# The second attention's GpSimd work and transfers in program order, its features loaded in fours ahead of time

## The chip, the core and the metric

The kernel runs on one core of one Trainium2 chip. The metric is the device time of one execution in microseconds, as the median of three runs. The profile comes from one more execution, recorded by the hardware profiler.

## What is computed

Two layers, each with a layer norm, an attention and a mixture of experts whose output gates the attention (`x = x + attention * silu(experts)`), on `x` of 4 batches x 512 tokens x 128. The change touches the second attention only. It has 16 heads of 8 features, and runs the same softmax attention under 16 "channels", which scale the scores of each head by another number:

```python
def wl_step(acc, wl):
    cpm, iw = wl
    m = cpm[None, :, None, None]
    Qw = Q * m
    Kw = K * m
    scores = jnp.einsum('bhqd,bhkd->bhqk', Qw, Kw) * SCALE
    scores = scores * jnp.cos(KERR * scores * scores)
    attn = jax.nn.softmax(scores, axis=-1)
    out = jnp.einsum('bhqk,bhkd->bhqd', attn, V)
    return (acc + out * iw, None)
acc, _ = jax.lax.scan(wl_step, acc0, (cos_pm, interference_weights))
combined = acc / WL_CHANNELS
```

The kernel does not take 16 exponentials of each score. It writes each channel's exponential as a combination of six functions of the unscaled score `s`: three exponentials `e`, `e*e`, `e*e*e` (bank 0), and `s*s`, `s` and 1 (bank 1). Summed over the keys, bank 0 needs every score. Bank 1 does not: sums over keys of `s` and `s*s` are products of q's features (its 8 numbers, their squares, and their pairwise products) with sums over the keys ("forms") that are made once a batch.

## The kernel before

**Stages.** A first norm and its experts (up to about 80 us), the first attention (to about 400 us), the second experts `ffn1` (to 531 us), and then the loop of the second attention, `attn1` (L1542), to the end.

**The loop.** It has 64 steps `i`: batch `b = i // 16`, and in a batch `t = i % 16`; `m = t // 4` is a group of four heads, `k = t % 4` a quarter of the keys. In a step TensorE makes the scores of step `i + 1` (`scores1`, tile `s`, 8 matmuls in bf16) and adds step `i`'s three exponentials into `acc` (12 matmuls, tile `acc`). ScalarE makes `e` and its square from the scores, VectorE the third power (L1531). At `t % 4 == 0` VectorE empties `acc` into bank 0 (L1573). Other matmuls lie between: the mixing of batch `b` and `b - 1` (function `mixing`, L1576: `bank1` at t = 4, 8, 12, 15, `sums1`, `quotients1`, and `output1` of the batch before at t = 9), and the preparation of batch `b + 1` (`prepare1`, L1155: token projections at t = 0, 1, 13, `project` of k and q at t = 2 and 3, forms at t = 5, 7, 10, 11). What is multiplied in one step is evicted and finished (`rest`) in the next.

**Where the operands come from.** `project("k")` and `project("q")` leave k and q with features on partitions. GpSimd splits each into three bf16 parts (L1247, L1250), SyncE writes the parts to DRAM (`kd`, `qd`, L1255) in eight places, which make up the pairs of parts that are multiplied with each other (`MEET`); `operands1` (L1288) reads them back, one group m at a time, with the parts stacked on the partitions: four transfers of 128 KB a group, three buffers each. q itself is written to DRAM twice (L1241), so that `features1` (L1298) can read it shifted by d features: for each m two loads of `rows1` (L1304), four of `rows2` (L1309) and four of `other` (L1310), each 64 KB, and then two products on GpSimd: `rows1`'s second half squared (L1305), and `rows2 * other` (L1311). `bank1(b, m)` multiplies the forms with `rows1` and `rows2`. There is one buffer of `other`, and one place in `rows1` and `rows2` for each m.

**GpSimd's other work in the loop**: the squares of the tokens (L1190), the keys' features `feat` for the forms (L1195 to L1205), the sum of the two products of a group (L1381), the output's gate and residual (L1400, L1401), and the experts' gate (`gate1`, L985 and L986, called at t = 2). ScalarE, VectorE and TensorE each write or read what GpSimd makes: `sizes` reduces the squares on VectorE, `output1` on TensorE takes the sums of L1381.

**What sets the order.** Each engine and SyncE's queue take their instructions one after the other. The order of TensorE, ScalarE and VectorE is the program's own: `mm1`, `act1` and `vec1` call `pin`, which is `keep_in_program_order`. GpSimd's instructions and the transfers are not pinned; the scheduler places them. `features1` is called for all four m at t = 0 of the batch (t = 1 in the first):

```python
if t == int(b == 0):
    if b == 0:
        nc.gpsimd.memset(self.rows1[64:65], 1.0)
    for m in range(4):
        self.features1(b, m)
```

Of the kernel before, what the change touches and what calls it, by code (L numbers as in the profile page):

```python
# [21 lines left out]
P = 128  # L22
# [44 lines left out]

MEET = (((0, 0), (0, 1), (1, 0), (1, 1)), ((0, 2), (2, 0), (1, 2), (2, 1)))

# [20 lines left out]
class Kernel:  # L90
# [124 lines left out]
    def load_second(self, pool):  # L215
# [3 lines left out]
        for w in ("q", "k", "v"):  # L219
            self.w1[w] = pool.tile([P, D], F32, name=f"l1w{w}")  # L220
            nc.sync.dma_start(out=self.w1[w], in_=i[f"L1_attn_W{w}"])

            flat = pool.tile([P, D], F32, name=f"l1b{w}f")
            nc.gpsimd.dma_start(out=flat, in_=i[f"L1_attn_b{w}"].partition_broadcast(P))
            self.wt[w] = pool.tile([P, D], F32, name=f"l1w{w}t")
            self.bt[w] = pool.tile([P, D], F32, name=f"l1b{w}t")
            for to, src in ((self.wt[w], self.w1[w]), (self.bt[w], flat)):
                nc.gpsimd.tensor_copy(
                    to.rearrange("p (m r d) -> p m r d", m=4, r=4),
                    src.rearrange("p (r m d) -> p m r d", m=4, r=4),  # L230
                )
            if w != "v":
                self.b1[w] = pool.tile([P, 1], F32, name=f"l1b{w}")
                nc.gpsimd.dma_start(out=self.b1[w], in_=i[f"L1_attn_b{w}"].unsqueeze(1))
        self.b1["o"] = pool.tile([P, D], F32, name="l1bo")
# [80 lines left out]
    def vec1(self, ins):  # L316
        return self.pin(ins)


# [661 lines left out]
    def gate1(self, pool, acc, name):  # L981

        t = pool.tile([P, 4, D], F32, name=f"th{name}", tag="pr1", bufs=2)
        self.act1(t, acc, AF.Tanh, scale=0.5)
        self.nc.gpsimd.tensor_scalar(t, t, 0.5, 0.5, ALU.mult, ALU.add)  # L985
        self.nc.gpsimd.tensor_mul(acc, acc, t)  # L986

# [167 lines left out]
    def prepare1(self, b, xnT, psum, tag):  # L1155
# [9 lines left out]
        def tokens(w):  # L1165
# [9 lines left out]
            def rest(ps):  # L1175
                if w == "v":
                    self.vec1(nc.vector.tensor_tensor(
                        strip[:, :, :, 18:26], ps.rearrange("p k (h d) -> p k h d", d=D1),
                        bc(self.bt[w].rearrange("p (h d) -> p h d", d=D1), 1, 4), ALU.add,
                    ))  # L1180
                    return
                twice = pool.tile([P, 4 * H1, 2 * D1], F32, name=f"tok{w}{b}", tag="tok")
                t = twice[:, :, 0:D1]
                self.vec1(nc.vector.tensor_tensor(
                    t.rearrange("p (k h) d -> p k h d", k=4),
                    ps.rearrange("p k (h d) -> p k h d", d=D1),
                    bc(self.bt[w].rearrange("p (h d) -> p h d", d=D1), 1, 4), ALU.add,
                ))
                sq = pool.tile([P, 4 * H1, D1], F32, name=f"tsq{w}{b}", tag="tsq")
                nc.gpsimd.tensor_mul(sq, t, t)  # L1190
                now["squares" + w] = sq
                if w == "q":
                    return
                fours = "p (g r) d -> p g r d"
                nc.gpsimd.tensor_copy(  # L1195
                    self.feat[:, :, 0:32].rearrange("p g (r d) -> p g r d", r=4),
                    t.rearrange(fours, r=4),
                )
                nc.gpsimd.tensor_copy(
                    self.feat[:, :, 32:64], sq.rearrange("p (g r) d -> p g (r d)", r=4)  # L1200
                )
                nc.gpsimd.tensor_copy(twice[:, :, D1 : 2 * D1], t)
                for d in range(1, 5):
                    at = ROWS1 + 32 * (d - 1)
                    nc.gpsimd.tensor_mul(  # L1205
                        self.feat[:, :, at : at + 32].rearrange("p g (r d) -> p g r d", r=4),
                        t.rearrange("p (g r) d -> p g r d", r=4),
                        twice[:, :, d : d + D1].rearrange("p (g r) d -> p g r d", r=4),
                    )
            return pe, rest  # L1210
# [12 lines left out]
        def project(w):  # L1223
            def pe():
                ps = psum.tile([P, S], F32, name=f"pj{w}{b}", tag=tag[0], bufs=tag[1])
                self.mm1(ps, lhsT=self.w1[w], rhs=toks, start=True, stop=True)
                return ps
# [6 lines left out]
            def rest(t):  # L1234
                if w == "q":

                    dram = now["dram"] = self.a1d.tile(
                        [H1, 2 * D1, S], F32, name=f"qd{b}", tag="qd"
                    )
                    for k in range(2):  # L1240
                        nc.sync.dma_start(out=dram[:, k * D1 : (k + 1) * D1, :], in_=t)  # L1241
                dram = now["parts" + w] = self.a1d.tile(
                    [H1, 2, 4, D1, S], BF16, name=f"{w}d{b}", tag=f"{w}d"
                )
                for k in range(3):
                    part = pool.tile([P, S], BF16, name=f"part{w}{b}_{k}", tag=f"part{k}")
                    nc.gpsimd.tensor_copy(part, t)  # L1247
                    if k < 2:
                        left = pool.tile([P, S], F32, name=f"left{w}{b}_{k}", tag="left", bufs=2)
                        nc.gpsimd.tensor_sub(left, t, part)  # L1250
                        t = left
                    for x in range(2):
                        for i, pair in enumerate(MEET[x]):
                            if pair[w == "k"] == k:
                                nc.sync.dma_start(out=dram[:, x, i], in_=part)  # L1255
            return pe, rest, evict
# [31 lines left out]
    def operands1(self, b, m):  # L1288

        nc, now = self.nc, self.now1[b]  # L1290
        for w in ("q", "k"):
            src = now["parts" + w].rearrange("(r m) x i d s -> m x r (i d) s", m=4)[m]
            for x in range(2):
                t = self.a1q.tile([P, S], BF16, name=f"{w}{x}_{b}_{m}", tag=f"{w}{x}", bufs=3)
                nc.sync.dma_start(out=t, in_=src[x])
                now[w, x, m] = t

    def features1(self, b, m):  # L1298

        nc = self.nc  # L1300
        src = self.now1[b]["dram"].rearrange("(r m) j s -> m r j s", m=4)[m]
        one, two = self.rows1[:, m], self.rows2[:, m]
        for k in range(2):
            nc.sync.dma_start(out=one[k * 32 : k * 32 + 32], in_=src[:, 0:D1])  # L1304
        nc.gpsimd.tensor_mul(one[32:64], one[32:64], one[32:64])  # L1305
        other = self.a1q.tile([P, S], F32, name=f"other{b}_{m}", tag="other", bufs=1)
        for d in range(1, 5):
            rows = slice(d * 32 - 32, d * 32)
            nc.sync.dma_start(out=two[rows], in_=src[:, d : d + D1])  # L1309
            nc.sync.dma_start(out=other[rows], in_=src[:, 0:D1])  # L1310
        nc.gpsimd.tensor_mul(two, two, other)  # L1311

# [44 lines left out]
    def quotients1(self, b, mm, x):  # L1357
# [15 lines left out]
        def rest(out):  # L1373
            for o in range(2):
# [5 lines left out]
                else:  # L1380
                    self.nc.gpsimd.tensor_add(self.prod1[b, m], self.prod1[b, m], t)  # L1381
        return pe, rest

    def output1(self, b, g1):
# [12 lines left out]
        def rest(po):  # L1397
            y = self.a1.tile([P, 4, D], F32, name=f"y{b}", tag="pr1", bufs=2)
            self.vec1(nc.vector.tensor_tensor(y, po, bc(self.b1["o"], 1, 4), ALU.add))
            nc.gpsimd.tensor_mul(y, y, g1[b])  # L1400
            nc.gpsimd.tensor_add(y, y, self.x[:, b * 4 : b * 4 + 4, :])  # L1401
            for k in range(4):
                nc.sync.dma_start(out=self.tiles_of(self.out, b * 4 + k), in_=y[:, k])
        return pe, rest

    def large1(self, flag):
# [5 lines left out]
        def first():  # L1412
# [3 lines left out]
            ))  # L1416
            nc.gpsimd.partition_all_reduce(every, bounds, P, bass_isa.ReduceOp.max)

# [16 lines left out]
    def end1(self, b, g1):  # L1435
# [4 lines left out]
        x = self.x[:, b * 4 : b * 4 + 4, :]  # L1440
        nc.gpsimd.tensor_mul(y, g1[b], bc(self.b1["o"], 1, 4))
        nc.gpsimd.tensor_add(y, y, x)
        den = psum.tile([P, 4, P], F32, name="dene", tag="prep")
# [36 lines left out]
        def output(k):  # L1480
# [10 lines left out]
            self.vec1(v.tensor_add(y[:, k], r, y[:, k]))  # L1491
            nc.sync.dma_start(out=self.tiles_of(self.out, b * 4 + k), in_=y[:, k])

# [48 lines left out]
    def attn1(self, xnT, g1):  # L1542
# [4 lines left out]
        with tc.tile_pool(name="a1", bufs=2) as self.a1, tc.tile_pool(  # L1547
# [47 lines left out]
            third = function(0, 2, self.e1)  # L1595
            waiting, late, prep = [], [], {}
            large = self.large1(flag)
            for i in range(n):
                b, t = i // 16, i % 16
                if t == 2:  # L1600
                    self.gate1(pool, g1[b], b)
# [5 lines left out]
                if t == 0:  # L1607
                    prep = self.prepare1(b + 1, xnT, psum, ("prep", 1)) if b + 1 < B else {}
                if t == int(b == 0):
                    if b == 0:  # L1610
                        nc.gpsimd.memset(self.rows1[64:65], 1.0)
                    for m in range(4):
                        self.features1(b, m)
                nxt = i + 1 < n
# [453 lines left out]
```

## Time and profile before

| | us |
|---|---|
| three runs, median | 927.83 |
| three runs, lowest and highest | 924.93 and 927.9 |
| the profiled execution, its own time | 925.29 |
| its span, from the first to the last instruction | 923.6 |
| TensorE busy (matmuls) | 855.1 (93% of the span) |
| VectorE busy | 595.7 (65%) |
| ScalarE busy | 519.6 (56%) |
| GpSimd busy | 382.5 (41%) |
| start of the second attention's loop | 531.4 |
| mean granted TensorE clock | 0.973 of full speed |

How to read what follows: PE is TensorE, PEld its weight loads, DVE VectorE, ACT ScalarE, POOL GpSimd, and SPq SyncE's queue of transfers. An instruction is named by its line and by what it writes and reads, "out<-in"; a line can be that of a helper, so that all matmuls stand at L311, all activations at L314. In a timeline, the first two numbers are start and duration, and the bracket at the end is the idle time of the engine ahead of the instruction and what ended it. Instructions in GpSimd's or SyncE's queue are not counted as busy while they issue transfers or wait.

### The profile page before, as it was taken

The numbers are of one execution on the slowest core, as the hardware profiler recorded it, in microseconds if no ns is written. First come the engines' busy times: TensorE is split into PE (matmuls) and PEld (weight loads), VectorE is DVE, ScalarE is ACT, GpSimd is POOL, SyncE is SP. The second block draws the span as 40 slices with busy tenths as digits, with TensorE's granted clock in tenths as the row PEclk, the third lists the DMA queues.
The fourth block names the chain that finished last, engine by engine and source line by source line (L and its number), as shares of the span: only waits on it lengthen the run. The fifth ranks groups of instructions, "written<-read, shape, count | busy, mean of one in ns | idle before, by whom it ended". The sixth has DMA issues, their size and how long they took to land. (4 is left out here: it accounts for less than half of the span.)

```text
span 923.6 us, 19255 instructions
## 1 busy us (share of the span) xinstructions
PE 855.1 (93%) x7660; PEld 528.9 (57%) x7660; DVE 595.7 (65%) x1202; ACT 519.6 (56%) x692; POOL 382.5 (41%) x465
## 2 busy tenths in 40 slices
PE   8998999999999999999999999496968999889996
PEld 4665789888898788866777733132325323422324
DVE  7863776676768788733534377364764786586675
ACT  3434564575656756524332497374853878388780
POOL 7730254544544345640330076313854284432112
PEclk9999999999999999999999999797997999899999
DMA  8402221211212121000041011521142214220000
GB/s 214 126 13 76 80 76 25 81 48 48 80 25 81 27 68 36 1 1 1 1 144 51 1 36 61 158 90 64 39 144 85 71 39 146 83 69 32 1 12 16
DMA packets 76705, 56.60 MB, mean 61 GB/s; under 512 B 40337, under 2 KB 65201, under 8 KB 76609
## 3 DMA queue, kind: packets, MB, share of 16 engines
q1 hardware_dynamic: 74608, 53.89, 19.4%
q0 software_dynamic: 1424, 1.16, 0.6%
q8 instruction: 62, 1.02, 0.4%
q10 hardware_dynamic: 576, 0.26, 0.1%
q14 instruction: 35, 0.28, 0.1%
HBM read 35.36 MB, written 19.92 MB: 60 GB/s over the span
## 5 line engine op out<-in xcount | busy, mean ns | idle before, releaser
L1531 DVE TENSOR_TENSOR e<-e,e 128x1024 f32<-128x1024 f32 x126 | 181.0, 1476 | 85.4 <-ACT e L314 85.3
L311 PE MATMUL acc<-e,strip 128*32 128x512 f32 x1520 | 185.9, 606 | 15.6 <-DVE bank L1573 8.2
L314 ACT ACTIVATE e<-s 128x1024 f32<-128x1024 f32 x126 | 122.1, 1022 | 106.3 <-PE s L311 106.3
L314 ACT ACTIVATE e<-e 128x1024 f32<-128x1024 f32 x126 | 126.3, 1060 | 0.0
L311 PEld LDWEIGHTS acc<-e,strip 128*32 128x32 f32 x1520 | 44.9, 110 | 128.6 <-issue 87.0
L314 ACT ACTIVATE h<-ph 128x1024 f32<-128x1024 f32 x32 | 32.7, 1023 | 87.8 <-PE ph L311 87.8
L311 PEld LDWEIGHTS eo<-w_out,h 128*128 128x128 f32 x512 | 61.7, 194 | 11.7 <-issue 10.4
L314 ACT ACTIVATE pj<-pp 128x512 f32<-128x512 f32 x64 | 38.1, 596 | 49.3 <-PE pp L311 49.3
L311 PE MATMUL eo<-w_out,h 128*128 128x128 f32 x512 | 64.0, 279 | 1.0 <-DVE g L958 0.8
L759 POOL TENSOR_TENSOR t<-t,gate 128x512 f32<-128x512 f32 x32 | 40.8, 1275 | 56.1 <-DVE t L692 41.5
L958 DVE SCALAR_TENSOR_TENSOR g<-eo,gw,g 128x128 f32<-128x128 f32 x112 | 31.5, 345 | 48.7 <-PE eo L311 48.7
L311 PE MATMUL ph<-xnT,w_in 128*128 128x512 f32 x128 | 61.2, 600 | 0.0
L311 PE MATMUL dot<-vone,E 128*128 128x65 f32 x512 | 61.1, 273 | 0.0
L311 PEld LDWEIGHTS dot<-vone,E 128*128 128x128 f32 x512 | 59.8, 192 | 1.1 <-issue 0.8
L711 POOL TENSOR_TENSOR t<-t,gate 128x512 f32<-128x512 f32 x32 | 41.0, 1280 | 33.3 <-DVE t L692 33.3
L1305 POOL TENSOR_TENSOR rows<-rows 32x512 f32<-32x512 f32 x16 | 18.2, 1139 | 86.8 <-DMA rows<-qd 63.7
L311 PE MATMUL s<-q,k 32*128 32x512 bf16 x512 | 39.7, 383 | 13.0 <-DMA k<-kd 11.7
L734 DVE TENSOR_TENSOR mz<-mz,mu 64x512 f32<-64x512 f32 x56 | 38.3, 685 | 18.3 <-PE mu L311 17.7
L654 DVE SCALAR_TENSOR_TENSOR elu<-elu,up 128x512 f32<-128x512 f32 x60 | 42.4, 707 | 7.2 <-ACT up L314 6.4
L760 POOL TENSOR_TENSOR t<-t,t 128x512 f32<-128x512 f32 x32 | 45.8, 1430 | 2.5
L1311 POOL TENSOR_TENSOR rows<-rows,other 128x512 f32<-128x512 f32 x16 | 25.1, 1570 | 49.2 <-DMA other<-qd 20.1
L630 DVE TENSOR_TENSOR E<-sc,cap 128x1024 f32<-128x1024 f32 x32 | 39.0, 1220 | 9.6 <-PE sc L311 7.0
(279 smaller groups left out, 1618.6 us busy)
## 6 DMA issues: line engine op xcount, KB each, us to landing
vd<-vt SPq DMA_DIRECT2D x32, 256.0 KB
vone<-vd SPq DMA_DIRECT2D x64, 128.0 KB
rows<-qd SPq DMA_DIRECT2D x96, 64.0 KB
kd<-partk SPq DMA_DIRECT2D x32, 128.0 KB
qd<-partq SPq DMA_DIRECT2D x32, 128.0 KB
k<-kd SPq DMA_DIRECT2D x32, 128.0 KB
q<-qd SPq DMA_DIRECT2D x32, 128.0 KB
other<-qd SPq DMA_DIRECT2D x64, 64.0 KB
```

The costliest lines, as they stand in the source:

```text
L311: return self.pin(self.nc.tensor.matmul(*args, **kw))
L314: return self.pin(self.nc.scalar.activation(*args, **kw))
L630: self.vec1(nc.vector.tensor_tensor(e.rearrange("p x hp c -> p (x hp) c"), ps.rearrange("p x hp c -> p (x hp) c"), bc(self.cap.rearrange(" ...
L654: self.vec1(nc.vector.scalar_tensor_tensor(t, t, 1.0, up, ALU.min, ALU.add))
L711: nc.gpsimd.tensor_mul(t, t, self.gate)
L734: self.vec1(nc.vector.tensor_tensor(new[half, :, :, p, 0:DK], old[half, :, :, p, 0:DK], ps[half, :, :, p * 64 : p * 64 + 64].rearrange("d ...
L759: nc.gpsimd.tensor_mul(t, t, gate2)
L760: nc.gpsimd.tensor_add(t, t, seg[n]["t1"])
L958: self.vec1(v.scalar_tensor_tensor(acc[b][:, k, :], eo[:, k, :], w, acc[b][:, k, :], ALU.mult, ALU.add))
L1305: nc.gpsimd.tensor_mul(one[32:64], one[32:64], one[32:64])
L1311: nc.gpsimd.tensor_mul(two, two, other)
L1531: self.vec1(self.nc.vector.tensor_mul(t, src[0][pair], src[1][pair]))
```

## The change

All GpSimd instructions and all transfers of the second attention are pinned to program order (`pool1`, `dma1`). The features of group m are loaded at t = 9, 11, 13 of the batch before (m = 0, 1, 2) and at t = 1 of the batch (m = 3); in the first batch at steps 1 to 4. Their two products are issued at the beginning of the step two later (one later in the first steps). q is written to DRAM a third time, once unduplicated (`once`), and features come by one load of `rows1` and one of `other` that repeat the same rows, so 6 transfers for 10. Parts are written with one transfer for all places that take the same part and lie evenly (`STAND`), 5 for each of q and k in place of 8, and operands are read with one transfer for both stacks, 2 for 4. For that the heads stand in another order: the projections use the permuted weights `wt`, and the permuted bias comes in 4 small loads for each of q and k. The gate is at t = 11 instead of 2.

```diff
+STAND = {
+    "q": (((0, 0, 4, 2), (1, 0, 1, 1)), ((0, 1, 4, 2), (1, 1, 2, 1)), ((1, 2, 4, 1),)),
+    "k": (((0, 0, 2, 1), (1, 2, 3, 1)), ((0, 2, 4, 1), (1, 3, 4, 1)), ((1, 0, 2, 1),)),
+}
...
             if w != "v":
                 self.b1[w] = pool.tile([P, 1], F32, name=f"l1b{w}")
-                nc.gpsimd.dma_start(out=self.b1[w], in_=i[f"L1_attn_b{w}"].unsqueeze(1))
+                own = i[f"L1_attn_b{w}"].rearrange("(r m d o) -> m r d o", m=4, r=4, o=1)
+                for m in range(4):
+                    nc.gpsimd.dma_start(out=self.b1[w][m * 32 : m * 32 + 32], in_=own[m])
...
+    def pool1(self, ins):
+        return self.pin(ins)
+
+    def dma1(self, out, in_):
+        return self.pin(self.nc.sync.dma_start(out=out, in_=in_))
...
-                self.mm1(ps, lhsT=self.w1[w], rhs=toks, start=True, stop=True)
+                self.mm1(ps, lhsT=self.wt[w], rhs=toks, start=True, stop=True)
...
-                    dram = now["dram"] = self.a1d.tile(
+                    once = now["once"] = self.a1d.tile([P, S], F32, name=f"qe{b}", tag="qe")
+                    self.dma1(once, t)
+                    twice = now["twice"] = self.a1d.tile(
                         [H1, 2 * D1, S], F32, name=f"qd{b}", tag="qd"
                     )
                     for k in range(2):
-                        nc.sync.dma_start(out=dram[:, k * D1 : (k + 1) * D1, :], in_=t)
+                        self.dma1(twice[:, k * D1 : (k + 1) * D1, :], t)
                 dram = now["parts" + w] = self.a1d.tile(
-                    [H1, 2, 4, D1, S], BF16, name=f"{w}d{b}", tag=f"{w}d"
+                    [2, P, 4, S], BF16, name=f"{w}d{b}", tag=f"{w}d"
                 )
...
-                    for x in range(2):
-                        for i, pair in enumerate(MEET[x]):
-                            if pair[w == "k"] == k:
-                                nc.sync.dma_start(out=dram[:, x, i], in_=part)
+                    for x, at, end, step in STAND[w][k]:
+                        n = len(range(at, end, step))
+                        self.dma1(dram[x, :, at:end:step], bc(part, 1, n))
...
-        for w in ("q", "k"):
-            src = now["parts" + w].rearrange("(r m) x i d s -> m x r (i d) s", m=4)[m]
+        for w in ("k", "q"):
+            src = now["parts" + w].rearrange("x (m r d) i s -> m (r d i) x s", m=4, r=4)[m]
+            t = self.a1q.tile([P, 2, S], BF16, name=f"{w}_{b}_{m}", tag=f"{w}s", bufs=3)
+            self.dma1(t, src)
             for x in range(2):
-                t = self.a1q.tile([P, S], BF16, name=f"{w}{x}_{b}_{m}", tag=f"{w}{x}", bufs=3)
-                nc.sync.dma_start(out=t, in_=src[x])
-                now[w, x, m] = t
+                now[w, x, m] = t[:, x]
 
     def features1(self, b, m):
 
-        nc = self.nc
-        src = self.now1[b]["dram"].rearrange("(r m) j s -> m r j s", m=4)[m]
+        nc, now = self.nc, self.now1[b]
+        once, twice = now["once"][m * 32 : m * 32 + 32], now["twice"][m * 4 : m * 4 + 4]
         one, two = self.rows1[:, m], self.rows2[:, m]
-        for k in range(2):
-            nc.sync.dma_start(out=one[k * 32 : k * 32 + 32], in_=src[:, 0:D1])
-        nc.gpsimd.tensor_mul(one[32:64], one[32:64], one[32:64])
+        self.dma1(one[0:64], bc(once, 0, 2))
         other = self.a1q.tile([P, S], F32, name=f"other{b}_{m}", tag="other", bufs=1)
         for d in range(1, 5):
-            rows = slice(d * 32 - 32, d * 32)
-            nc.sync.dma_start(out=two[rows], in_=src[:, d : d + D1])
-            nc.sync.dma_start(out=other[rows], in_=src[:, 0:D1])
-        nc.gpsimd.tensor_mul(two, two, other)
+            self.dma1(two[d * 32 - 32 : d * 32], twice[:, d : d + D1])
+        self.dma1(other, bc(once, 0, 4))
+
+        def products():
+            self.pool1(nc.gpsimd.tensor_mul(one[32:64], one[32:64], one[32:64]))
+            self.pool1(nc.gpsimd.tensor_mul(two, two, other))
+        return products
...
-            waiting, late, prep = [], [], {}
+
+            steps = {9: 0, 11: 1, 13: 2, 1: 3}
+
+            def features(b, t):
+
+                out = [(0, t - 1)] if b == 0 and 1 <= t < 5 else []
+                if t in steps and (b, t) != (0, 1):
+                    out.append((b + (t > 1), steps[t]))
+                return out
+            waiting, late, prep, products = [], [], {}, []
...
-                if t == 2:
+                if t == 11:
                     self.gate1(pool, g1[b], b)
...
-                if t == int(b == 0):
-                    if b == 0:
-                        nc.gpsimd.memset(self.rows1[64:65], 1.0)
-                    for m in range(4):
-                        self.features1(b, m)
+                while products and products[0][0] <= i:
+                    products.pop(0)[1]()
+                if i == 1:
+                    self.pool1(nc.gpsimd.memset(self.rows1[64:65], 1.0))
+                for fb, m in features(b, t):
+                    if fb < B:
+                        products.append((i + (1 if i < 5 else 2), self.features1(fb, m)))
```

Every other GpSimd instruction of the second attention (L985, L986, L1190 to L1209, L1247, L1250, L1381, L1400, L1401, L1417, L1441, L1442) is wrapped in `pool1`, and the output's transfers are issued by `dma1`.

## The prediction

> **What bounds the kernel now.** I read the page's busy shares first, then the waits, then TensorE's timeline and the queue's beside it. TensorE is busy 93% of the span, so the question is what keeps it from the other 7%. The waits from 531 us (start of the second attention's loop) to the end are few and long (us in total, times, longest):
>
> ```profile
> ACT e L314 <- PE s L311: 106.3, 46, 18.1
> PE po L311 <- POOL pr L1381: 15.7, 4, 11.1
> PE s L311 <- DMA k<-kd: 11.7, 2, 10.9
> PE acc L311 <- DVE bank L1573: 8.2, 8, 2.3
> PE acc L311 <- DVE e L1531: 7.3, 2, 7.0
> ```
>
> In TensorE's timeline (start, duration, instruction, idle before it) these are single places:
>
> ```profile
> 596.30 0.61 PE L311 MATMUL s<-q,k 32*128 32x512 bf16 x4 [10.93 <-DMA k<-kd]
> 638.78 1.92 PE L311 MATMUL acc<-e,strip 128*32 128x512 f32 x4 [7.01 <-DVE e L1531]
> 695.62 0.80 PE L311 MATMUL po<-wo_rep,pr 128*128 128x128 f32 x2 [11.09 <-POOL pr L1381]
> 696.84 5.74 PE L311 MATMUL po<-wo_rep,pr 128*128 128x128 f32 x26 [0.42 <-POOL pr L1381]
> 787.70 0.80 PE L311 MATMUL po<-wo_rep,pr 128*128 128x128 f32 x2 [2.82 <-POOL pr L1381]
> 789.90 5.31 PE L311 MATMUL po<-wo_rep,pr 128*128 128x128 f32 x26 [1.41 <-POOL pr L1381]
> ```
>
> Each ends at work of SyncE's queue or GpSimd that stands in a bad order. At 585 to 596 the operands of group 3 (L1295) are issued behind eighteen part and q transfers of the next batch (576.28 to 589.4); at 690 the sum that the output waits for (L1381) stands on GpSimd behind a feature product whose load has only just been issued; at 632 a vector reduction waits 9.93 us for squares (L1190) that stand behind feature products. The queue before the stall of 695.62:
>
> ```profile
> 682.82 1.37 SPq L1304 DMA_DIRECT2D rows<-qd  x2
> 684.29 0.60 SPq L1309 DMA_DIRECT2D rows<-qd  x1
> 684.93 0.60 SPq L1310 DMA_DIRECT2D other<-qd  x1
> ...
> 688.79 0.60 SPq L1310 DMA_DIRECT2D other<-qd  x1
> ```
>
> And the stretches by time (TensorE, weight loads, VectorE, ScalarE, GpSimd, granted clock, DMA share, GB/s):
>
> ```profile
> 590.00:600.00 10.00, 2.94 (x20) 0.69 (x24) 0.00 (x0) 1.68 (x2) 0.00 (x0) 0.50 0.29 95
> 690.00:700.00 10.00, 3.96 (x17) 3.66 (x18) 0.00 (x0) 0.00 (x0) 3.70 (x3) 0.50 0.27 97
> 720.00:730.00 10.00, 10.00 (x88) 3.29 (x84) 6.16 (x7) 7.94 (x9) 3.81 (x3) 1.00 0.14 49
> ```
>
> In a stall all engines stand still and the clock is 0.50; elsewhere TensorE is full at 1.00 and no other engine is near its limit.
>
> **What the Trainium skill says.** (1) "DMA: Bandwidth & Descriptors", Anatomy of one DMA: a wait for a semaphore happens on the issuing sequencer before dispatch, so a waiting transfer holds all behind it. The trace agrees: the queue's own waits show 12 of L1310 for GpSimd's product, 48.2 us. (2) Same page, Rules for kernel authors: a leading broadcast of c copies confines a transfer to at most c of the 16 engines. No broadcast load of this kind is in the trace, but feature loads, whose source leads with 4 heads, hold the DMA share at 0.27, or 4.3 engines, with 97 GB/s: some 23 GB/s each. (3) "SBUF — State Buffer", Who interferes with whom: a VectorE operation with two SBUF inputs and a GpSimd one that reads SBUF exclude each other. The trace agrees: the product e takes 1226 ns in the median and up to 2332. (4) "TensorE: Matmul & The Clock Gate", What's actually happening: after an idle window of about 3.4 us the clock is half. Above: 0.50 behind both long stalls.
>
> **The yardstick.** I took the start of each step's score matmuls (s, x8) as the step's start; a step does scores and 12 accumulations. Step 9, with nothing else, goes from 575.00 to 578.25: 3.25 us. Added work from the chain's undisturbed rows: token projections 1.09 (three a batch), projections 1.07 (two), forms pl 1.49 (four), bank b 1.92 (four), den 1.87, mix 1.06, po 3.77. So batch 1 needs 16 x 3.25 + 11.37 + 19.43 = 82.8 us, and takes 624.97 to 733.92 = 108.95, 26.1 too long. Batch 2: 92.8, 10.0 too long. Batch 0, without den, mix and po of a predecessor: needs 75.0, takes 93.55, 18.5 too long. Together 54.6. Five steps hold most of it:
> - step 10 (578.25 to 596.30): 18.05 for 3.25 + 1.87 + 1.49 = 6.6: 11.4
> - step 11 (to 604.91): 8.61 for 4.7: 3.9 (the slow clock: its accumulation took 5.28, not 2.78)
> - step 17 (629.31 to 646.47): 17.16 for 3.25 + 1.09 + 1.87 = 6.2: 10.9
> - step 25 (680.57 to 702.51): 21.94 for 3.25 + 3.77 = 7.0: 14.9
> - step 41 (780.91 to 795.14): 14.23 for 7.0: 7.2
>
> Sum 48.3. The other 6.3 of these batches and some 7 in batch 3 are short waits for VectorE.
>
> **The change part by part.**
> - **GpSimd and SyncE in program order; features of m = 0, 1, 2 at t = 9, 11, 13 of the batch before and m = 3 at t = 1, products two steps later.** I followed each queue for batch 1, from the start of t = 1, with durations under contention (page and groups). GpSimd: token products from 2.7 us on, 11.5 long (L1190 1.37, L1195 1.62, L1199 1.28, L1202 0.61, four of L1205 at 1.67), to 14.2; products of m = 3 (1.14 + 1.57), to 16.9; the splits of k 6.0 and q 6.6 and gaps 1.5, to 31; the sums L1381 2 x 1.55, with their input ready at 32, to 35. The output matmuls come at 43.8: 9 us of margin. Forms need the token products at 23.5, ready at 14.2. SyncE waits for the splits up to 31, then issues group 3's operands, landing by 36, wanted at 54. The gate moves from t = 2 to 11; its two products (1.28 + 1.93) lie between y and m = 0's product, and are wanted a batch later. The all-reduce of batch 3 (L1417, idle 9.33 ahead of it) stays between m = 3's product at t = 3 and the sums at t = 7, four steps on: 0. The out transfers stand ahead of the features at t = 11 and wait for y; that costs the queue 8 us, and features of m = 1 still land 1.5 us after their slot at t = 13, where only GpSimd waits. So all five long steps go: **-48.3**.
> - **Broadcast loads.** `one` 128 KB, four `two` of 64 KB, `other` 256 KB: 6 issues for 10. Not in the trace. Lower bound: on all 16 engines at 23 GB/s, 640 KB take 1.7 us. Upper bound: `one` on two engines, the rest on four, engines 0 and 1 carry 64 + 64 + 64 KB: 8.3 us and some 2 of latency. I take the upper one: against 9.7 us or more of two steps it costs GpSimd about a microsecond at times, inside the margin. **0**; if the margin were gone, 1 us a set.
> - **Fewer issues.** Per batch 78 become 49 (features 40 to 24, parts 16 to 10, operands 16 to 8, q 2 to 3) at 0.6 us: 17 us less of SyncE, which TensorE doesn't see: 0, but it lets the queue run ahead. One copy of q more, 256 KB a batch: hidden at 0.14 to 0.3 DMA share.
> - **Batch 0 is tight**, since its four sets go out at steps 1 to 4. GpSimd's token products (538.9 on) now stand ahead of the first feature product, which ended at 550.98 in between: they end at about 550.8, the products at 553.8. Bank 0's second half could start at 551.03: **+2.4**. After that each `other` (one buffer) waits for the last product; the splits fill these gaps; q's last parts leave at 576, group 3's operands land near 581 and are wanted near 586: **+0.5** for the small margin. GpSimd stays busy to 579, so products e stretch in some steps of 3.25 us: **+1.5**.
> - **VectorE loses its rest.** Batch 1's first steps waited 0.2 us after a long stall, batch 2's 2.4 (steps 32 to 36). Batch 1 will look like batch 2: **+2.3**.
> - **At the start**, two biases load in 4 pieces each: 6 more issues on GpSimd at 0.55 = 3.3 us around 15 to 37 us. GpSimd waits 16.0 us at L1130 later: 0 (bounds 0 to 3.3 if the phases' load delays VectorE at 47 us). The permuted weights already exist.
>
> Sum: -48.3 + 2.4 + 0.5 + 1.5 + 2.3 = -41.6. The profiled execution took 925.29 (span 923.6 and 1.7 around it): 883.7. The runs' median, 927.83, lies 2.5 above it, but one of three was below, so I add half: **885**.
>
> **The rivals.**
> - **A: a wait takes the place of the removed ones.** In order, GpSimd waits for a load with splits and sums behind it. Against: 9 us of margin. For: batch 0, and one buffer for `other`. One stall like step 41's per boundary, 2 or 3 x 7: 885 + 18 = 903.
> - **VectorE becomes the bound**: half of a batch's 16 pairs e at 3.5 to 4 us, not 2.4, in steps of 3.25 to 4.3: another 2 to 3 us a batch, 885 + 8 = 893. Against: VectorE is 65% busy.
> - **Slower than before**: the broadcast loads are so slow that every set arrives late. From 9.7 + 9 = 19 us a set (twice my upper bound) TensorE sees it; at 23 us each of 15 sets costs about 3.7, that is 55: 885 + 55 = 940. The 0.27 share with 97 GB/s speaks against it.
> - **The order was not the cause**: the stalls stay for their bytes, 921. At 585 to 596 the share is 0.47, at 686 to 695 0.24, so bytes don't bind.
>
> **Numbers.** Forecast 0.70, A 0.15, VectorE 0.10, slower 0.03, no effect 0.02. Its own range is 876 (nothing of the +6.7 comes, 877.0, and a microsecond of the old short waits goes too) to 893. To 899 it takes in the VectorE case and half of A, and leaves less than 2 in 10. A measurement of this kernel tells about 0.3% from no change. Faster 0.96, within 0.01, slower 0.03.
>
> **What would show it.** Right: no wait of TensorE over 3 us between 531 us and the end; `s` from `k<-kd` and `po` from `pr` gone; clock 1.00 throughout; the loop from its start to the last bank some 332 us for 373. Bank 0 of batch 0 waits 2 us for `rows`. The DMA share in feature loads about 0.2. Wrong: `po` or `b` waits for GpSimd at each batch (A), many short waits for e or bank on VectorE, or a stretch ahead of 531 us that is longer.

## The result and the profile after

| | before | after |
|---|---|---|
| median | 927.57 (4 runs, 924.93 to 927.9) | 889.78 (4 runs, 887.72 to 891.24) |
| ratio, 95% interval | | 0.9597 [0.957, 0.9624] |
| the profiled execution | 925.29 | 890.56 |
| its span | 923.6 | 888.8 |
| start of the loop | 531.42 | 534.06 |
| loop, from the start of step 0 to that of step 62 | 364.2 | 326.6 |
| mean granted clock | 0.973 | 0.992 |

The change is 37.8 us faster in the median; the forecast was 885, so it is 4.8 us short. In the new kernel all lines have moved: matmuls stand at L318, activations at L321, the third power `e` at L1548, bank 0 at L1590, the two products of a group at L1324 and L1325, the sums at L1397, and every pinned transfer at L330.

TensorE's main waits in the new kernel from the loop's start to the end, with two of ScalarE and GpSimd (us in total, times, longest), the counterpart of the first view of the prediction:

```profile
ACT e L321 <- PE s L318: 69.0, 47, 3.5
POOL rows L1325 <- DMA other<-qe: 23.3, 6, 5.1
PE acc L318 <- DVE bank L1590: 10.4, 9, 2.3
PE b L318 <- POOL rows L1324: 1.4, 1, 1.4
PE acc L318 <- DVE e L1548: 1.3, 4, 0.5
PE b L318 <- POOL rows L1325: 1.1, 1, 1.1
```

Before, TensorE waited here for `pr`, `k<-kd`, `bank` and `e`, 11 us at the longest. Now `pr` and `k<-kd` are gone, and no wait of TensorE is longer than 2.3 us. What remains is VectorE: `bank` 10.4 us in nine waits, which stands behind products `e` in VectorE's order. GpSimd waits 23.3 us for `other`; TensorE waits for GpSimd only 1.4 and 1.1 us, at step 4, where the product that it wants stood behind other work and not behind a load.

The same stretches of time as before (columns as in the prediction: TensorE, weight loads, VectorE, ScalarE, GpSimd, clock, DMA share, GB/s):

```profile
590.00:600.00 10.00, 10.00 (x89) 3.76 (x89) 7.18 (x15) 8.15 (x9) 2.47 (x3) 1.00 0.32 98
690.00:700.00 10.00, 9.71 (x78) 2.98 (x76) 8.76 (x8) 7.94 (x9) 3.40 (x3) 1.00 0.38 94
720.00:730.00 10.00, 9.10 (x70) 2.44 (x65) 9.78 (x7) 8.08 (x10) 9.63 (x8) 1.00 0.24 79
```

The two stalls, where TensorE was busy 2.94 and 3.96 us of 10, are full. At 720 to 730 the next limit can be seen: VectorE 9.78 and GpSimd 9.63 us of 10, TensorE 9.10.

### The profile page after: what moved, and what is told of

It reads as the page before. It is cut to its first block, busy times and chain, and to the rows that moved or that the text cites. A ratio compares the mean times of both kernels' runs of the same rounds, so it can differ in the third digit from the quotient of the medians.

```text
span 888.8 us, 19127 instructions
## 1 busy us (share of the span) xinstructions
PE 850.0 (96%) x7660; PEld 525.9 (59%) x7660; DVE 596.3 (67%) x1202; ACT 520.1 (59%) x692; POOL 383.4 (43%) x471
## 5 line engine op out<-in xcount | busy, mean ns | idle before, releaser
L1548 DVE TENSOR_TENSOR e<-e,e 128x1024 f32<-128x1024 f32 x126 | 182.2, 1486 | 78.1 <-ACT e L321 78.1
L318 PE MATMUL acc<-e,strip 128*32 128x512 f32 x1520 | 185.0, 601 | 11.8 <-DVE bank L1590 10.4
L321 ACT ACTIVATE e<-s 128x1024 f32<-128x1024 f32 x126 | 122.1, 1022 | 69.0 <-PE s L318 69.0
L321 ACT ACTIVATE e<-e 128x1024 f32<-128x1024 f32 x126 | 126.4, 1060 | 0.0
L318 PEld LDWEIGHTS acc<-e,strip 128*32 128x32 f32 x1520 | 44.9, 110 | 125.5 <-issue 86.6
L321 ACT ACTIVATE h<-ph 128x1024 f32<-128x1024 f32 x32 | 32.8, 1024 | 87.5 <-PE ph L318 87.4
L318 PEld LDWEIGHTS eo<-w_out,h 128*128 128x128 f32 x512 | 62.5, 196 | 11.7 <-issue 10.4
L321 ACT ACTIVATE pj<-pp 128x512 f32<-128x512 f32 x64 | 38.2, 597 | 50.4 <-PE pp L318 50.2
L318 PE MATMUL eo<-w_out,h 128*128 128x128 f32 x512 | 64.5, 281 | 1.0 <-DVE g L971 0.8
L318 PE MATMUL dot<-vone,E 128*128 128x65 f32 x512 | 61.1, 273 | 0.0
L318 PEld LDWEIGHTS dot<-vone,E 128*128 128x128 f32 x512 | 59.8, 192 | 1.1 <-issue 0.8
L318 PE MATMUL ph<-xnT,w_in 128*128 128x512 f32 x128 | 60.3, 594 | 0.0
L321 ACT ACTIVATE attT<-pa 128x512 f32<-128x512 f32 x32 | 19.1, 597 | 46.2 <-PE pa L783 46.2
L740 POOL TENSOR_TENSOR mz<-mz,zs 64x8 f32<-64x8 f32 x56 | 11.7, 209 | 70.3 <-DVE zs L672 61.6
L321 ACT ACTIVATE E<-E 128x1024 f32<-128x1024 f32 x32 | 33.6, 1051 | 11.5 <-DVE E L643 11.5
```

Of the source, the lines that this page charges most:

```text
L318: return self.pin(self.nc.tensor.matmul(*args, **kw))
L321: return self.pin(self.nc.scalar.activation(*args, **kw))
L740: nc.gpsimd.tensor_add(new[half, :, :, p, DK].rearrange("d hp a -> d (hp a)"), old[half, :, :, p, DK].rearrange("d hp a -> d (hp a)"), seg ...
L1548: self.vec1(self.nc.vector.tensor_mul(t, src[0][pair], src[1][pair]))
```

## The experiments

All experiments start from the changed kernel; each diff shows what is different from it. "Too long" is the prediction's measure, a step's time less 3.25 us and less the matmuls added to it. Ratios are to the kernel before, run on the same chip, where its medians were 923.3 to 926.8.

### The parts of the change: the early features, the two orders, the sizes

**The pins without the early features.** All four groups are loaded and multiplied at the start of the batch, as before, and the gate is back at t = 2:

```diff
-                if t == 11:
+                if t == 2:
...
-                for fb, m in features(b, t):
-                    if fb < B:
-                        products.append((i + (1 if i < 5 else 2), self.features1(fb, m)))
+                if t == int(b == 0):
+                    for m in range(4):
+                        self.features1(b, m)()
```

> The changed kernel with its pins and its larger transfers, but all four feature sets of a batch loaded and multiplied at t = 0 (t = 1 in the first batch) and the gate at t = 2, as before. My theory (the pins need the moved features: in order, GpSimd waits for four loads one after the other, 10 + 3 x 8 = 34 us, with the token products, splits and sums behind them): forms and output wait 15 to 20 us in each of batches 1 and 2 and some in batch 0, so 930 to 955 us. Rival (the order by itself was the gain, the place of the features not): 888 to 895 us. Rival (the larger transfers were the gain): also 888 to 895.

Measured: 921.2 us, 0.9956 [0.9936, 0.9977]. It is 9 us better than its range: I expected a kernel slower than before, and it is 0.4% faster. Both rivals (888 to 895) are ruled out. The old stalls are gone, and others stand in their place. In its waits and its timeline:

```profile
PE pl L318 <- POOL feat L1212: 16.2, 1, 16.2
PE pl L318 <- POOL feat L1218: 14.3, 3, 5.4
```

```profile
569.46 1.26 POOL L1325 TENSOR_TENSOR rows<-rows,other 128x512 f32<-128x512 f32 x1 [5.39 <-DMA other<-qe]
...
572.89 1.09 PE L318 MATMUL pl<-strip,feat 128*65 128x36 f32 x8 [16.20 <-POOL feat L1212]
```

The fourth group's product waits 5.39 us for its `other`, as each group's did, since there is one buffer; the token products behind it in program order, which begin at 570.67, and the forms `pl` behind those, come 16.2 us late. Pinning a queue in which waiting loads stand first makes an order that is fixed and bad. The gate, which is back at t = 2 too, stands behind the token products here (577.69), so this wait owes nothing to it; what it adds elsewhere is not separated in this run. (It is tried by itself below.)

**The early features without the pins.**

```diff
     def pool1(self, ins):
-        return self.pin(ins)
+        return ins
 
     def dma1(self, out, in_):
-        return self.pin(self.nc.sync.dma_start(out=out, in_=in_))
+        return self.nc.sync.dma_start(out=out, in_=in_)
```

> The changed kernel without the pins on GpSimd and the transfers: features moved, transfers larger, the scheduler orders both queues again. My theory (both the place and the order carry the gain; the scheduler pulls products and loads ahead of what TensorE waits for): 895 to 910 us, with one or two waits of TensorE over 3 us. Rival (the place of the features and the fewer transfers were all of it): 888 to 892 us. Rival (the order alone is the gain): 920 or more.

Measured: 913.66 us, 0.9871 [0.9819, 0.9922], a little above the range. Two of the old stalls are back, step 17 (10.3 too long) and step 25 (7.6), and a new one stands at step 4 (9.1; it was 0.4 before), where TensorE waits for a feature product that the scheduler put behind the token products. In GpSimd's timeline and TensorE's around step 17:

```profile
630.50 1.03 POOL L1324 TENSOR_TENSOR rows<-rows 32x512 f32<-32x512 f32 x1 [7.84 <-DMA rows<-qe]
633.10 1.26 POOL L1325 TENSOR_TENSOR rows<-rows,other 128x512 f32<-128x512 f32 x1 [1.57 <-DMA rows<-qd]
634.32 1.04 POOL L1203 TENSOR_TENSOR tsqq<-tokq 128x512 f32<-128x512 f32 x1
635.39 0.69 DVE L1228 TENSOR_REDUCE sizeq<-tsqq 128x64 f32<-128x512 f32 x1 [9.14 <-POOL tsqq L1203]
637.72 1.92 PE L318 MATMUL acc<-e,strip 128*32 128x512 f32 x4 [6.23 <-DVE e L1548]
```

This is the prediction's stall of 632 us, here with its full chain: the scheduler has put the squares `tsqq` behind a product whose load is still on its way (7.84 and 1.57 us), VectorE's reduction waits 9.14 us for them, `e` stands behind the reduction, and TensorE waits 6.23 us for `e`.

So all but the pins is worth 1.3%, all but the early features and the gate's place 0.4%, and everything together 4%: 13 and 6 us apart, 38 together. Each half needs the other. (The 6 are with the gate at t = 2, which costs 7.9 us in the changed kernel, see below. Even with all of that added the two halves would make 27.)

**The transfers pinned, GpSimd not** (only `pool1` without its pin).

> The changed kernel with the transfers pinned and GpSimd's instructions not. My theory (one of the two old stall kinds was SyncE's order, the other GpSimd's): between moved alone and the change, 890 to 900 us; what is left are waits for sums or token products on GpSimd. Rival (only SyncE's order matters): 888 to 892 us.

Measured: 903.35 us, 0.9749 [0.969, 0.9807], above the range. TensorE's waits for GpSimd in it:

```profile
PE po L318 <- POOL pr L1397: 8.7, 4, 2.9
PE b L318 <- POOL rows L1325: 5.0, 1, 5.0
```

Step 4 and both outputs at t = 9 are 6.8 to 7.8 us too long.

**GpSimd pinned, the transfers not** (only `dma1` without its pin).

> The changed kernel with GpSimd's instructions pinned and the transfers not; the scheduler holds group 3's operands of a batch back to the end of the part transfers, as before. My theory: like the change but for late loads; 890 to 900 us, with the output's wait for sums at t = 9 (7 to 8 us in each of batches 1 and 2 where only the transfers were pinned) gone. Rival (each pin alone gives half of what both give): 900 to 905 us.

Measured: 884.69 us, 0.958 [0.9532, 0.9627], better than the range. None of the long waits comes back, although SyncE's order is the scheduler's. So with GpSimd in order, pinning the transfers as well gains nothing. It is not worthless by itself: with GpSimd unpinned, pinned transfers took the kernel from 913.66 to 903.35. I ran GpSimd's pins once more, beside the change itself:

> Only GpSimd's instructions pinned, once more. If pinning the transfers costs something (the collisions at t = 15 and t = 0 that pinned loads bring about): 882 to 887 us, 3 to 6 below the change run beside it. Rival (the first difference was chance): within 2 us of the change.

> The changed kernel once more, beside the next run on the same chip. All theories: 886 to 892 us.

Measured: 885.93 us, 0.9589 [0.9558, 0.9619], and for the change 888.4, 0.9614 [0.9583, 0.9645]. The loop is 321.5 us against 326.7 in the profiles (323.1 against 326.6 for the earlier runs of the two), so twice it is shorter with the transfers left free. The medians are 2.5 us apart in this pair, between what the two theories expected, and the intervals of their ratios overlap: that free transfers are better is likely, and not settled.

**As many transfers as before**, with all else of the change:

```diff
-                        n = len(range(at, end, step))
-                        self.dma1(dram[x, :, at:end:step], bc(part, 1, n))
+                        for j in range(at, end, step):
+                            self.dma1(dram[x, :, j], part)
...
-            self.dma1(t, src)
             for x in range(2):
+                self.dma1(t[:, x], src[:, x])
...
-        self.dma1(one[0:64], bc(once, 0, 2))
+        for k in range(2):
+            self.dma1(one[k * 32 : k * 32 + 32], once)
...
-        self.dma1(other, bc(once, 0, 4))
+        for k in range(4):
+            self.dma1(other[k * 32 : k * 32 + 32], once)
```

> The changed kernel with as many transfers as before (parts one place each, operands 128 KB each, features 10 for 6), pinned and at the changed places. My theory (SyncE's issue time lies off the path, the margin of the moved features covers 17 us of issues a batch): 888 to 893 us, and the first batch loses 1 to 3 us since its chain of feature loads is longer by 4 x 0.6 us a set. Rival (fewer and larger transfers carry a part of the gain): 900 us or more.

Measured: 890.69 us, 0.9628 [0.9574, 0.9682]; the loop is 325.6 us against 326.6. Fewer and larger transfers are worth nothing that can be seen.

The permuted heads and the third copy of q are in all of these runs, so what they cost or gain by themselves is not measured.

### The remainder: which short waits, and whose

**GpSimd's products cut to 8 of 512 columns.** This leaves the rest of the features unmultiplied, to see what the products cost others; all waits and loads stay.

```diff
-            self.pool1(nc.gpsimd.tensor_mul(one[32:64], one[32:64], one[32:64]))
-            self.pool1(nc.gpsimd.tensor_mul(two, two, other))
+            self.pool1(nc.gpsimd.tensor_mul(one[32:64, 0:8], one[32:64, 0:8], one[32:64, 0:8]))
+            self.pool1(nc.gpsimd.tensor_mul(two[:, 0:8], two[:, 0:8], other[:, 0:8]))
```

> The changed kernel with both feature products cut to 8 of 512 columns (the rest of the features stays unmultiplied). My theory (the 1.3 us that steps t = 15 and t = 0 of batches 1 and 2 take too long, and the 2.9 us at step 4, come from GpSimd's products: they hold up the products e on VectorE and bank 0 of the first batch): step 4 under 0.8 us too long, steps 15 and 0 under 0.5 each, the loop 5 to 9 us shorter, 881 to 886 us. Rival (VectorE is late at t = 15 and t = 0 by its own products with the banks, and step 4 waits for something else): the loop within 2 us of the change.

Measured: 880.07 us, 0.9527 [0.9483, 0.9572]; the loop is 315.9 us, 10.7 less. That is better than its range. Step 4 falls from 2.86 too long to 0.96. At the seams of the batches, the 1.33 of t = 15 goes to nothing, and the 1.31 of t = 0 falls to 0.87 only. Step 48 gives 2.1 of the 10.7, of which 1.7 are a difference of the clock that may be chance (last section). The first seam, steps 31 and 32 of the change, in VectorE's, GpSimd's and TensorE's timeline:

```profile
695.20 1.03 POOL L1324 TENSOR_TENSOR rows<-rows 32x512 f32<-32x512 f32 x1
695.25 4.30 DVE L1548 TENSOR_TENSOR e<-e,e 128x1024 f32<-128x1024 f32 x2 [1.24 <-ACT e L321]
697.14 1.32 POOL L1325 TENSOR_TENSOR rows<-rows,other 128x512 f32<-128x512 f32 x1 [0.91 <-DMA other<-qe]
...
700.22 3.48 POOL L1397 TENSOR_TENSOR pr<-pr,pr 128x512 f32<-128x512 f32 x2 [1.75 <-DVE pr L1392]
700.66 4.12 DVE L1548 TENSOR_TENSOR e<-e,e 128x1024 f32<-128x1024 f32 x2
704.70 0.68 DVE L1590 COPY bank<-acc 128x512 f32<-128x512 f32 x1
705.43 2.78 PE L318 MATMUL acc<-e,strip 128*32 128x512 f32 x24 [1.24 <-DVE bank L1590]
```

A pair of `e` takes 2.36 us alone. Here the pair of 695.25 takes 4.30 beside the two products of m = 2, and that of 700.66 takes 4.12 beside the sums. `bank`, next in VectorE's order, is late by as much, and TensorE waits 1.24 us for it. In the cut kernel the same places:

```profile
690.33 2.36 DVE L1548 TENSOR_TENSOR e<-e,e 128x1024 f32<-128x1024 f32 x2 [1.25 <-ACT e L321]
...
694.64 3.45 DVE L1548 TENSOR_TENSOR e<-e,e 128x1024 f32<-128x1024 f32 x2 [0.76 <-ACT e L321]
698.75 2.78 PE L318 MATMUL acc<-e,strip 128*32 128x512 f32 x24 [0.80 <-DVE bank L1590]
```

The first pair is back at 2.36 (the second, beside the sums, is not, which is why t = 0 keeps 0.87), and the wait for the bank is 0.80. The kernel with free transfers shows it in another way, with its products whole: there the larger product of m = 2 starts only 0.3 us before the end of the next pair, and that pair takes 2.36.

```profile
696.83 2.36 DVE L1548 TENSOR_TENSOR e<-e,e 128x1024 f32<-128x1024 f32 x2 [0.76 <-ACT e L321]
698.92 1.41 POOL L1325 TENSOR_TENSOR rows<-rows,other 128x512 f32<-128x512 f32 x1 [2.64 <-PE b L318]
```

**The first feature product ahead of the token products**, so that bank 0 isn't late at step 4:

```diff
+                if i == 1:
+                    products.pop(0)[1]()
```

> The changed kernel with the first feature products of batch 0 ahead of the token products at step 1. My theory (bank 0 at step 4 waits for the feature products only because they stand behind the token products): step 4 loses its 2.9 us, forms at step 5 stay covered or wait up to 1 us; the loop 1.5 to 2.5 us shorter, 887 to 889 us. Rival (the wait is for the loads, or moves to the forms): no difference, or step 5 gets the 2 to 3 us.

Measured: 889.19 us, 0.9619 [0.9574, 0.9664], no gain. Step 4 falls from 2.86 too long to 0.86 as meant, but step 10 rises from 1.54 to 4.86, with a wait that the change doesn't have:

```profile
PE s L318 <- DMA q<-qd: 3.1, 1, 3.1
```

The first product waits for its loads on GpSimd (4.46 and 3.89 us of idle time ahead of its two halves), all work behind it is later, the splits of q too, and so are group 3's operands. It is the small margin of batch 0 that the prediction priced at 0.5: 8.35 us of idle time on GpSimd come out as 3.3 on TensorE at step 10, and as 1.6 more at step 11, where matmuls ran slow behind the wait.

**A version put together from these**: the first product ahead, the products of m = 2 one step later, and `one` and `other` loaded from plain rows.

```diff
+                if i == 1:
+                    products.pop(0)[1]()
...
-                        products.append((i + (1 if i < 5 else 2), self.features1(fb, m)))
+                        products.append((i + (1 if i < 5 else 3 if m == 2 else 2), self.features1(fb, m)))
```

> The changed kernel with the first products ahead, the products of m = 2 one step later (t = 0 for t = 15), and the repeated loads of rows1 and other as two and four plain loads, which may run on all 16 DMA engines. My theory: GpSimd's 23 us of waits for other nearly vanish and TensorE doesn't see that; steps 15 and 0 lose 1 to 2 us together in each of batches 0 to 2; the loop 3 to 6 us shorter than the change, 884 to 888 us. Rival (the collisions only move by a step): as the run with the first products ahead.

Measured: 885.71 us, 0.9586 [0.9538, 0.9633], in its range. For the most part the collisions only moved, as its rival said: steps 31 and 47 are no longer too long, but step 16 is by 1.72, and step 32 by 1.72 in place of 1.31. The second, with free transfers, the first product ahead and plain rows, and m = 2 where it was:

> Only GpSimd pinned, the first products ahead of the token products, and plain loads in place of the repeated ones. If both single gains add up (3.5 us of the loop from free transfers, 2 at step 4): 880 to 884 us. Rival (with the first products ahead the splits of q end later and group 3's operands arrive late at step 10 or 11, as in the run with the first products ahead): no better than GpSimd's pins alone.

Measured: 885.03 us, 0.9585 [0.9556, 0.9614], above its range and no better than GpSimd's pins alone (885.93 on the same chip). The gains don't add: step 4 falls to 1.15 too long, but the products of m = 2 meet `e` again (1.32 and 1.31 at the seams), likely because plain rows land earlier.

**The gate back at t = 2**, all else as in the change (the line `if t == 11:` alone).

> The changed kernel with the gate at t = 2 again. My theory (the gate's place is of no account: 3 us of GpSimd inside its margin of 9 us to the output matmuls): 887 to 893 us. Rival (at t = 2 it stands between the token products and the splits, and the output or the forms wait): 2 to 3 us a batch more, 895 to 900 us.

Measured: 896.3 us, 0.9721 [0.9683, 0.9758], 7.9 more than the change on the same chip: the rival's range, not mine. In its timeline:

```profile
549.07 2.12 POOL L999 TENSOR_TENSOR g<-g,th 128x512 f32<-128x512 f32 x1
551.26 1.91 POOL L1324 TENSOR_TENSOR rows<-rows 32x512 f32<-32x512 f32 x1
553.22 4.28 PE L318 MATMUL b<-rows,lin 65*128 65x512 f32 x4 [5.21 <-POOL rows L1324]
557.43 3.79 PE L318 MATMUL acc<-e,strip 128*32 128x512 f32 x24
```

The gate's two products (the second is shown) stand ahead of the first feature product, and bank 0's step waits 5.21 us for that in place of 1.44. Behind the wait the granted clock is 0.50 (553.2 to 557.4), and the matmuls of `b` and `acc` take 4.28 and 3.79 us, where 1.99 and 2.78 are usual. So step 4 is 8.58 too long, 5.7 more than in the change. The loop of this profiled execution is 7.3 us longer than that of the change measured beside it (334.0 against 326.7), which is nearly all of the 7.9. The two profiled executions differ by less, 894.98 and 891.56, because the loop starts at 529.76 in one and at 534.93 in the other, with the same code ahead of it.

## Why the prediction was right, step by step

Set against its own sum (us too long in each batch of the loop, and how the forecast's terms fall on the batches):

| | before | forecast for after | after |
|---|---|---|---|
| batch 0 (steps 10 and 11; +2.4, +0.5, +1.5) | 18.5 | 7.6 | 6.1 |
| batch 1 (steps 17 and 25; +2.3) | 26.1 | 2.6 | 4.5 |
| batch 2 (step 41) | 10.0 | 2.8 | 4.4 |
| batch 3 (no change) | 6.9 | 6.9 | 9.0 |
| loop, change | | -41.6 | -37.6 |
| ahead of the loop | | 0 | +2.6 |

- **"So all five long steps go: -48.3"** held. Steps 11, 25 and 41 are not too long any more, step 17 is by 0.47 and step 10 by 1.54. From the loop's start to the last bank 0 it is 334.5 us for 372.1, where 332 for 373 was forecast. The cause held in part. That GpSimd's order made the stalls of steps 17, 25 and 41 is shown: with GpSimd unpinned, 17 and 25 return when the transfers are free, and 25 and 41 when they are pinned; with GpSimd alone pinned none does. That SyncE's order made the stall of step 10 fell: with the transfers in the scheduler's order and GpSimd pinned it doesn't come back. The kernel before shows another reading. In its timeline:

```profile
580.23 1.82 POOL L1311 TENSOR_TENSOR rows<-rows,other 128x512 f32<-128x512 f32 x1 [7.37 <-DMA kd<-partk]
582.00 0.61 POOL L1247 CAST partq<-qT 128x512 bf16<-128x512 f32 x1
583.59 5.79 SPq L1255 DMA_DIRECT2D qd<-partq  x8
587.55 0.61 POOL L1247 CAST partq<-leftq 128x512 bf16<-128x512 f32 x1
589.48 1.27 SPq L1295 DMA_DIRECT2D q<-qd  x2
```

  GpSimd stands idle for 7.37 us ahead of a feature product, the splits of q behind it end at 588.2, and the last parts go out just behind them, ahead of group 3's operands. The new kernel has the parts ahead of the operands too:

```profile
577.04 5.23 SPq L330 DMA_DIRECT2D qd<-partq  x5
582.43 0.37 SPq L330 DMA_DIRECT2D k<-kd  x1
```

  Counted from the loop's start the operands are issued 9.7 us earlier, though they stand behind the same parts. So the likelier cause is again GpSimd, whose splits came late; the run with the first product ahead shows that link at the same step. The runs with GpSimd unpinned don't test it, since TensorE had lost 9.1 and 6.8 us at step 4 already.
- **Batch 0's three terms** (+4.4) were right in sum, too dear by 1.5. The step-4 term can be checked by itself: bank 0's step was 0.40 too long before and is 2.86 now, +2.46 for the 2.4 forecast. "Bank 0 of batch 0 waits 2 us for `rows`": it waits 1.44 + 1.09. Step 10's 1.54 is more than the 0.5 for its margin; the other steps' short waits are 1.7 in all, where the sum left 18.5 - 15.3 - 0.4 + 1.5 = 4.3.
- **"VectorE loses its rest: +2.3"** came true where it was put: steps 16 to 20 were 0.3 too long together and are 2.7, beside 2.6 in steps 32 to 36. **What the sum left out is other steps**: t = 8 and t = 15 of batches 1 and 2 were hardly too long before, and are 0.48 and 1.33 now, 3.6 in the two batches together, for which the prediction had nothing. The mechanism is the one that the prediction cited: the Trainium skill's "SBUF — State Buffer", Who interferes with whom, has a VectorE instruction with two SBUF inputs and a GpSimd one that reads SBUF exclude each other, and the trace agrees, with pairs of `e` at 4.30 and 4.12 in place of 2.36. What I missed is the place: program order puts the two products of m = 2 at t = 15 and sums at t = 8 and t = 0, just ahead of VectorE's copy of the bank. With the products cut, t = 15 is no longer too long, and the 0.48 at t = 8, where a pair beside the sums takes 3.45, stays. Batches 1 and 2 then fall to 2.0 and 1.7 too long, 0.6 and 1.1 less than I forecast. The rival "VectorE becomes the bound" is thus true in part, some 3.6 us for its 8.
- **Batch 3, +2.1 for 0**, is mostly one accumulation at half clock behind a wait of 2.32 us, 1.7 us more than at full clock. The wait itself is not new: it was 2.34 before, with the accumulation at 2.78. Other executions with the wait don't all have the slow clock, so this part may be chance (last section). "Clock 1.00 throughout" was one of the signs of being right; it did not come, and at this place it is 0.61.
- **Ahead of the loop, +2.6 for 0.** The bias loads at the start, bounded at 0 to 3.3, can't be seen: the first projection of the first attention comes at 78.5 us, before at 78.0, and in the other executions with these loads at 77.7 to 78.6. Some 2.1 arise between 320 and 340 us, where the clock fell. In the experiments' executions the loop starts between 529.8 and 535.5 with the code ahead of it the same: at 529.8 to 532.1 where the clock is 1.00 from 330 to 340, and at 533.8 to 535.5 where it is 0.75 or less. So this is scatter between executions.
- **Broadcast loads and fewer issues: 0** held, with the transfers of before in place of them (890.69). The products that wait for `other` start 5.5 to 9.0 us after its issue (at 697.14 for 689.48, for one), inside the 10.3 of the upper bound; GpSimd's 23.3 us of waits for it are hidden.
- **The gate's place at 0** held for the change. But the prediction didn't say what the move avoids: with the gate left at t = 2 the pinned order costs 7.9 us, most of it at step 4.
- **Rival A** (a wait takes the place of the removed ones) and the slow loads did not come in the change, while A is just what the pins without the early features gave. "The order was not the cause, 921" is refuted by the pins of GpSimd, 913.66 to 884.69 with the transfers free in both.

In sum, 883.7 forecast for the profiled execution, and 4.0 from the loop and 2.6 from ahead of it make 890.3, for 890.56 measured. The median lies 0.8 below that execution, where I had added 1.3 to it. Some of the closeness is luck: batch 0 was priced 1.5 too dear, which hides part of the 3.6 that the sum left out.

## What to carry to other kernels

Fixing GpSimd's order paid little here until the transfers that it waits for were started well ahead: the two halves are worth 6 and 13 us apart, and 38 together. Pin the engine whose work others wait for and try the transfers apart; here GpSimd's pins alone gave all that both gave. When the long waits are gone, look at which VectorE and GpSimd instructions lie side by side just ahead of a result that TensorE wants, and expect that a wait shortened at one step comes back where the next margin is thin.

## What was not expected of the hardware

- **The clock halved behind a short wait, or without one.** In step 48, after 2.32 us:

```profile
792.61 4.44 PE L318 MATMUL acc<-e,strip 128*32 128x512 f32 x24 [2.32 <-DVE bank L1590]
```

  The same matmuls take 2.78 elsewhere, so 1.7 us are lost beside the wait. Six profiled executions have a wait of 2.32 us there: in four the matmuls take 4.44 to 4.48, and in two (as many transfers as before, and the second version put together) 2.78. So the same wait can bring the slow clock or not. And with TensorE full, in the first attention:

```profile
330.00:340.00 10.00, 10.00 (x96) 7.81 (x95) 8.25 (x26) 5.58 (x10) 2.12 (x2) 0.74 0.08 28
```

  The clock is 0.74 there, with TensorE busy throughout by the profile, and was 1.00 in this stretch before. The Trainium skill's "TensorE: Matmul & The Clock Gate", What's actually happening, has the clock fall after an idle window of about 3.4 us; these two places show it after less, so the measurement decides.
- **GpSimd waits longer with loads that repeat the same rows.** Ahead of the two products of a group GpSimd waits 43.6 us in 13 places for transfers in the change (`other` 23.3, `rows` 10.3 and 10.0). With plain transfers, two for `one` and four for `other`, it is 16.4 us in 6 places in the run with as many transfers as before, and 20.3 in 8 in the first version put together, though the queue has more to issue. These two runs differ from the change in other transfers or products as well, so not all of the difference need be the repeated rows. The loops of the change and of the former differ by 1.0 us, so TensorE sees hardly any of it.
